# One maximum, the last narrow passes and image 0's normalisation put into other places in an eight-image convolution sequence

## The chip, the cores and the metric

The kernel runs on one NeuronCore of a Trainium2 chip. What counts is device time in microseconds (us): the time of one execution on that core. Five engines run side by side, each with its own queue in program order, and meet only at semaphores: TensorE multiplies matrices into PSUM, VectorE and ScalarE do elementwise work, GpSimd does some sums in SBUF and issues small transfers, SyncE (SP) issues most DMAs. In the profile they are PE (PEld for its weight loads), DVE, ACT, POOL and SP.

## The reference

The input is 8 images of 512 channels and 32x32 positions, all in float32. Four layers follow one another:

```python
h = group_norm(x)                                   # layer 0: 8 groups of 64 channels
q, k, v = split(qkv_w @ h + qkv_b)
h = softmax(q k / 8) v                              # 8 heads of 64 channels
for _ in range(3): h = h + 0.1 * tanh(h @ inl_w.T + inl_b)
x = x + proj_w @ h + proj_b

x = x + softmax(Wq x . Wk x) (Wv x)                 # layer 1: one head over 1024 positions

x = upfirdn(x + bias, up=2)                         # layer 2: 12 taps, rows and columns
x = leaky_relu(x, 0.2) * sqrt(2)
x = upfirdn(x, down=2)

rw = sigmoid(mean(x) @ router_w.T + router_b)       # layer 3: 8 experts, weights mixed per image
W1, W2, W3 = mix(rw, w1), mix(rw, w2), mix(rw, w3)
y = relu(bn(conv1x1(x, W1))); y = relu(bn(conv3x3(y, W2)))
x = relu(bn(conv1x1(y, W3)) + x)
```

## The kernel before

Channels lie on the 128 partitions in 4 chunks (`CC`), positions on the free axis in two halves of 512 (`HALF`). Every wide product is done in Strassen's way with seven quarter products (`product`, L554, and `in_turn`, L610): P1, C11, U2, U3, C22, C21, C12. P1 and C11 read the left half of the positions as it is; U2, U3, C22 and C21 read four sums of quarters (`T_h`, made by `quarter_sum`, L541) and sums of the weights' quarters. An f32 matmul is one row in the code and two passes in the profile.

Layers 0 to 2 run image by image (loop at the end of the `weights` pool: `layer0`, `layer1`, `between`). Image 0 starts in `first_qkv` (L807): `channel_stats` (L419) takes `bn_stats` of each chunk as it lands, `norm_factors` (L441) averages mean and variance over groups with a tiny matmul each (`gn_mean`, `gn_var`), takes Sqrt on ScalarE and makes a factor and an addend per channel, and `group_norm` scales `x` chunk by chunk on VectorE. Then come the first sums of the query weights (`first_sums`, `first_rest`), the quarter sums, and q, k and v.

The order of work is set in two ways. Under `tc.manual_schedule(engines=...)` the named engines run what is issued in the order of the code. Elsewhere a planner orders the instructions by its own estimates; it also fills between two such blocks. `first_qkv` is left to the planner.

In the last image (b = 7) layer 0 also computes the router of images 0 to 6: `early_router` (L833) is a generator with a step for the sums on VectorE, one for `logits` (a matmul with ones, then seven VectorE steps and an exp on ScalarE) and one per image for the blend operators. The loop over 64 score tiles issues one step each time once i > 2 (L1010):

```python
                if i < steps:
                    scores(i)
                if i > 2:
                    next(router, None)
                if i >= lag:
                    weighted(i - lag)
```

Layer 2 of the last image is interleaved with layer 3 of images 0 and 1. `chain` is the generator `lean_images`: the first convolution in two halves (`first`, L1652), the spread of its rows for the 3x3 convolution (`spread`), the second convolution with 4 steps and the third with one step per output chunk `oc` (both in `second`, L1666). The third convolution's matmul results go to two PSUM banks of the pool `ps_mm`, and VectorE adds them onto `z` (L1700); a bank is free when that is done.

`fine_passes` (L1364) runs 8 row passes. Each has `up` (16 small matmuls into two PSUM pairs; ScalarE makes 0.2 times each pair, VectorE takes the maximum of both, L1292), `down` for the pass before (matmuls, then two copies to `sent`, on ScalarE, the second on VectorE in odd passes; SP stores `sent`), after the fourth `turn_back` (SP loads the stored rows as `back`), and then two calls of `fill`, each of which takes one step of `chain`. In the fifth pass the second `fill` also issues the loads of image 2 (`z`, 4 DMAs; `weights`, 12 DMAs), which `first(2, 0)` reads as c_2_0 (L1656).

`last_columns` (L1471) ends layer 2: for each half `e` of the channels two `narrow` passes (matmuls from `back`; copies on VectorE), steps of `chain`, and two `channels` (transposes zT; ScalarE copies them to `z` and sums the pooled mean). After it another hand-ordered block begins with image 2's first convolution (`c1`, c_2_1), its spread, the router of image 7 (`router.sums`) and c_3_0, and then loops over images 2 to 7. Between the two blocks the planner has put c_2_1, c_3_0 and five of the first six second-convolution matmuls between the last two narrow passes.

SP's queue is in program order: a store waits at its head for its copy, and the loads behind it wait too.

Of the kernel before, what the change touches and what calls it, by code (L numbers as in the profile page):

```python
# [9 lines left out]
F32 = mybir.dt.float32  # L10
BF16 = mybir.dt.bfloat16
AF = mybir.ActivationFunctionType
ALU = mybir.AluOpType
# [4 lines left out]
P = 128  # L18
B, C, H, W = 8, 512, 32, 32
S = H * W  # L20
# [38 lines left out]
def tile_sequence(ctx: ExitStack, tc: tile.TileContext, a: dict, out: bass.AP, shifted: bool):  # L59
# [359 lines left out]
    def channel_stats(b, x):  # L419

        stats = small.tile([P, CC, 2, 6], F32, tag="stats", bufs=1, name=f"stats_{b}")
        mv = small.tile([P, CC, 2], F32, tag="mv", bufs=2, name=f"mv_{b}")
        for cc in range(CC):
            for h in range(2):
                nc.vector.bn_stats(stats[:, cc, h, :], x[:, cc, ts(h, HALF)])
            nc.vector.bn_aggr(mv[:, cc, :], stats[:, cc, :, :].rearrange("p h s -> p (h s)"))
            yield mv
# [10 lines left out]
            nc.vector.tensor_sub(be, be, m)  # L438
            bn.append((g, be))

    def norm_factors(b, mv, made):  # L441
        mean_c, var_c = mv[:, :, 0], mv[:, :, 1]
        ps = ps_sc.tile([P, S], F32, tag="scores", name=f"gn_mean_{b}")
        nc.tensor.matmul(ps[:, 0:CC], group_mean, mean_c, start=True, stop=True)
        mean = small.tile([P, CC], F32, tag="gmean", bufs=2, name=f"gmean_{b}")
        nc.vector.tensor_copy(mean, ps[:, 0:CC])
        dev = small.tile([P, CC], F32, tag="gdev", bufs=2, name=f"gdev_{b}")
        nc.vector.tensor_sub(dev, mean_c, mean)
        nc.vector.tensor_mul(dev, dev, dev)
        nc.vector.tensor_add(dev, dev, var_c)  # L450
        yield
        ps = ps_sc.tile([P, S], F32, tag="scores", name=f"gn_var_{b}")
        nc.tensor.matmul(ps[:, 0:CC], group_mean, dev, start=True, stop=True)
        mul = small.tile([P, CC], F32, tag="gmul", bufs=2, name=f"gmul_{b}")
        nc.scalar.activation(mul, ps[:, 0:CC], AF.Sqrt, bias=eps)
        nc.vector.reciprocal(mul, mul)
        nc.vector.tensor_mul(mul, mul, gn_scale)
        add = small.tile([P, CC], F32, tag="gadd", bufs=2, name=f"gadd_{b}")
        nc.vector.tensor_mul(add, mean, mul)
        nc.vector.tensor_sub(add, gn_bias, add)  # L460
        made.extend((mul, add))
        yield

# [131 lines left out]
    def all_of(gen):  # L595
        for _ in gen:
            pass
# [207 lines left out]
        tc.keep_in_program_order(nc.scalar.activation(early, eps, AF.Exp))  # L805

    def first_qkv(h, w):  # L807
        made = []
        for mv in channel_stats(0, h):
            pass  # L810
        all_of(norm_factors(0, mv, made))
        group_norm(h, *made, nc.vector)
        first_sums(*held["q"], h[:, CC - 1, 0:1])
        t = quarter_sums("h_0", h)
        w["q"] = first_rest(*held["q"])
        for key in "kv":
            w[key] = weight_sums(key, *held[key], t[3][1][:, 0:1])
        q, parts = queries(0, h, t, w)
        all_of(parts)
        nc.vector.tensor_add(row_bias, row_bias, bias2)  # L820
        w["inl"] = weight("inl", 0)
        k, parts = keys(0, h, t, w)
        for _ in range(2):
            next(parts)
        early_exp(0)
        all_of(parts)
        w["proj"] = weight("proj", 0)
        v, parts = values(0, h, t, w)
        all_of(parts)
        w["v1"] = weight("v1", 0)  # L830
        return q, k, v
# [10 lines left out]
    def layer0(b, q, k, v, w):  # L842
# [162 lines left out]
        with tc.manual_schedule(engines={engines.PE, engines.DVE, engines.Activation}):  # L1005
            router = iter(early_router() if b + 1 == B else ())
            for i in range(steps + lag):
                if i < steps:
                    scores(i)
                if i > 2:  # L1010
                    next(router, None)
                if i >= lag:
                    weighted(i - lag)
                done = i - lag - SC - 1
                for g in range(1, 2 * PAIRS, 2):
                    closing_pair(g, done - g * SC)
                for g in range(2 * PAIRS, last_g):
                    closing(g, done - g * SC)
            t_hf = sum_tiles(f"hf_{b}_0")
            name = f"inl_{b}_0"  # L1020

            def last_total():
                quarter_sum(t_hf, hf, 0, (0, 1))
                for at in range(3):
                    closing(last_g, at)
                quarter_sum(t_hf, hf, 1, (0, 1))
                quarter_sum(t_hf, hf, 0, (2, 3))
                quarter_sum(t_hf, hf, 1, (2, 3))
# [208 lines left out]
    class Layer2:  # L1237
# [34 lines left out]
            for i in range(4):  # L1272
                nc.sync.dma_start(t[:, ts(i, 4), :], src[:, ts(i, 4), :])

        def up(self, e, i):

            n = 4 * e + i
            pairs = [
                ps_sc.tile([P, S], F32, tag="scores", name=f"up_{self.b}_{n}_{p}") for p in range(2)
            ]  # L1280
            for s in range(2):
                for g in range(4):
                    part = slice(W * g, W * g + W)
                    first = 4 * i + 2 * s
                    nc.tensor.matmul(  # L1285
                        pairs[g // 2][HD * s : HD * s + HD, ts(g % 2, HALF)], up_v[part, :],
                        self.turned[e][part, first : first + 2, :], start=True, stop=True,
                    )
            fine = self.fine[n] = [tmp(f"fine_{self.b}_{n}_{p}", S) for p in range(2)]
            for ps, t in zip(pairs, fine):  # L1290
                nc.scalar.mul(t, ps, 0.2)  # L1291
                nc.vector.tensor_max(t, ps, t)  # L1292

        def down(self, e, i):

# [67 lines left out]

        def fine_passes(self, fill):  # L1364
            order = [(e, i) for e in range(2) for i in range(4)]
            for n in range(len(order) + 1):
                if n < len(order):
                    self.up(*order[n])
                if n:
                    e, i = order[n - 1]  # L1370
                    self.down(e, i)
                    if i == 3:
                        self.turn_back(e)
                fill()
                fill()

    engines = mybir.EngineType
    hand = {engines.PE, engines.DVE, engines.Activation, engines.SP}
# [80 lines left out]
    def last_rows(two, chain, loads):  # L1459
        done = 0  # L1460

        def fill():
            nonlocal done
            next(chain, None)
            done += 1
            loads(done)

        with tc.manual_schedule(engines=hand):
            two.fine_passes(fill)

    def last_columns(b, two, chain, loads):  # L1471
        with tc.manual_schedule(engines=hand):
            z = big_tile(f"z_{b}", [P, CC, S])
            for e in range(2):
                two.narrow(e, 0)
                two.narrow(e, 1)
                loads(e)
                for _ in range(2):
                    next(chain, None)
                two.channels(e, 0, z)  # L1480
                two.channels(e, 1, z)
                for _ in range(4 - 2 * e):
                    next(chain, None)
            all_of(chain)
        return z

    def load_z(b):
        t = big_tile(f"z3_{b}", [P, CC, S])
# [177 lines left out]
    def second(b):  # L1666
# [14 lines left out]
        c2(b, main, 0, False, True)  # L1681
        nc.scalar.activation(h2[:, ts(0, HALF)], main, AF.Relu, bias=bn[1][1], scale=bn[1][0])
        transform_weights(b + 1)
        yield

        def closed(oc):
            dst = zs[b][:, oc, :]
# [3 lines left out]
        for oc in range(CC):  # L1691
            scale = bn[2][0][:, oc : oc + 1]
            apart = zs[b][:, oc, :].rearrange("p (n i) -> p i n", i=2)
            at = C + 12 * P + oc * P
            for i in (1, 0):
                ps = bank(name=f"c3_{b}_{oc}_{i}")
                nc.tensor.matmul(
                    ps, wts[b][:, at : at + P], h2[:, ts(i, HALF)], start=True, stop=True
                )
                nc.vector.scalar_tensor_tensor(  # L1700
                    apart[:, i], ps, scale, apart[:, i], ALU.mult, ALU.add
                )
            if oc:
                closed(oc - 1)
            yield
        closed(CC - 1)

    LEAN = 2
# [20 lines left out]
            load_image(3)  # L1729
            next(mixing)  # L1730

    zs[B - 1] = last_columns(B - 1, two, chain, more_loads)
    redo = None
    engines = mybir.EngineType
    with tc.manual_schedule(engines={engines.PE, engines.DVE, engines.Activation}):
        c1(LEAN, 1)
        spreads[LEAN] = spread(LEAN)
        router = Router(B - 1, 1)
        router.sums()
        c1(LEAN + 1, 0)  # L1740
        for b in range(LEAN, B):
            more = b + 1 < B
            if b + 2 < B:
# [110 lines left out]
```

## Time and profile before

| | us |
|---|---|
| median of 3 runs | 3546.42 (3546.16 to 3550.63) |
| profiled execution | 3549.11 |
| its span | 3547.3 |
| TensorE busy | 3508.9 |
| VectorE busy | 2320.8 |
| ScalarE busy | 1316.9 |
| mean granted TensorE clock | 0.998 |

The span counts from the first to the last instruction; some 1.8 us of the execution lie around it. In a row of the profile, `L585 PE` is line 585 on TensorE, followed by output and input tiles and sizes. In the timeline the first number is the start and the second the length; what stands in brackets is how long the engine had been idle before it and who ended that. In the list of waits the numbers are the total, how often, and the longest. TensorE's idle time in the whole span is 38 us, 11.0 of them before its first instruction.

### The profile page before, as it was taken

How to read it: one execution, taken by the hardware profiler on the slowest of the kernel's cores; microseconds unless marked ns; L12 is line 12 of the kernel's file. 1: busy time of each engine (PE TensorE's matmuls, PEld its weight loads, DVE VectorE, ACT ScalarE, POOL GpSimd, SP SyncE). 2: the span in 40 equal slices, each digit the busy share in tenths (PEclk: the TensorE clock that was granted, in tenths of full speed). 3: DMA queues.
4: the chain of work that ended last, by engine and by line, in shares of the span. 5: the costliest groups of instructions: out<-in, count | busy, mean ns of one | idle time of the engine just before them, and what ended most of it. 6: DMA issues, size and time to landing. Idle time of an engine off the chain costs nothing.

```text
span 3547.3 us, 48514 instructions
## 1 busy us (share of the span) xinstructions
PE 3508.9 (99%) x19649; PEld 1743.1 (49%) x19649; DVE 2320.8 (65%) x3131; ACT 1316.9 (37%) x1742; POOL 109.3 (3%) x152
## 2 busy tenths in 40 slices
PE   8999999999999999999999999999999999999998
PEld 4335643474435743465534744356434744347333
DVE  4787558765686557774677656775677656765544
ACT  0632346223442236323452235422462234531443
POOL 4100000000000000000000000000000000020000
PEclk9999999999999999999999999999999999999999
DMA  5112351115311341023411152013511153332783
GB/s 205 40 31 86 101 176 43 45 54 154 117 37 65 116 159 36 29 86 115 165 39 64 57 168 87 30 70 112 182 43 43 44 154 128 123 104 74 261 297 129
DMA packets 153841, 360.89 MB, mean 102 GB/s; under 512 B 20072, under 2 KB 94840, under 8 KB 147464
## 3 DMA queue, kind: packets, MB, share of 16 engines
q1 hardware_dynamic: 150104, 342.69, 29.1%
q0 software_dynamic: 3360, 14.75, 1.1%
q8 instruction: 156, 2.56, 0.3%
q14 instruction: 77, 0.63, 0.1%
q10 hardware_dynamic: 144, 0.26, 0.0%
HBM read 226.55 MB, written 118.49 MB: 97 GB/s over the span
## 4 chain that ended last, share of the span: by engine, by line
PE 96%; DMA 1%; DVE 1%; SPq 0%; ACT 0%; issue 0%; ACTq 0%; DVEq 0%
PE scores L872 12%; PE av L917 12%; PE inl_X L585 7%; PE av_X L1226 5%; PE inl_Y L585 5%; PE inl_A L585 5%; PE av_A L1226 3%; PE av_Y L1226 3%; PE v_X L585 3%; PE proj_X L585 2%; PE k_X L643 2%; PE q_X L643 2%; PE v_X L643 2%; PE c L1598 2%; PE v_Y L585 2%; PE v_A L585 2%
## 5 line engine op out<-in xcount | busy, mean ns | idle before, releaser
L891 ACT ACTIVATE e<-scores 128x1024 f32<-128x1024 f32 x504 | 516.7, 1025 | 395.4 <-PE scores L872 368.9
L872 PE MATMUL scores<-q,k 64*64 64x512 f32 x4096 | 530.7, 591 | 0.0
L917 PE MATMUL av<-e,v 64*64 64x512 f32 x4096 | 528.7, 589 | 0.0
L901 DVE TENSOR_TENSOR accs<-accs,e 128x1024 f32<-128x1024 f32 x240 | 294.3, 1226 | 49.6 <-ACT e L891 46.0
L917 PEld LDWEIGHTS av<-e,v 64*64 64x64 f32 x4096 | 156.5, 133 | 282.3 <-issue 274.0
L872 PEld LDWEIGHTS scores<-q,k 64*64 64x64 f32 x4096 | 152.8, 133 | 289.9 <-issue 255.6
L585 PE MATMUL inl_X<-T_hf,w_inl 128*128 128x512 f32 x576 | 262.3, 593 | 1.0 <-DVE inl_U L739 1.0
L1292 DVE TENSOR_TENSOR fine<-up,fine 128x1024 f32<-128x1024 f32 x128 | 150.8, 1220 | 105.4 <-ACT fine L1291 105.4
L1291 ACT ACTIVATE fine<-up 128x1024 f32<-128x1024 f32 x128 | 124.2, 1021 | 162.8 <-PE up L1285 161.6
L585 PEld LDWEIGHTS inl_X<-T_hf,w_inl 128*128 128x128 f32 x576 | 108.3, 190 | 141.4 <-issue 109.7
L585 PE MATMUL inl_A<-hf,w_inl 128*128 128x512 f32 x384 | 174.4, 597 | 0.0
L728 ACT ACTIVATE inl_U<-inl_U,inl_b 128x512 f32<-128x512 f32 x96 | 66.8, 719 | 287.3 <-DVE inl_U L743 287.3
L938 DVE RECIPROCAL inv<-av 128x256 f32<-128x256 f32 x80 | 139.0, 1745 | 0.0
L739 DVE TENSOR_TENSOR inl_U<-inl_X,inl_P 128x512 f32<-128x512 f32 x96 | 61.8, 686 | 106.6 <-PE inl_X L585 106.6
L899 DVE TENSOR_TENSOR accs<-e,e 128x1024 f32<-128x1024 f32 x48 | 59.6, 1243 | 99.5 <-ACT e L891 80.5
L1226 PE MATMUL av_A<-v,eT 128*128 128x256 f32 x512 | 122.6, 383 | 0.0
L585 PEld LDWEIGHTS inl_A<-hf,w_inl 128*128 128x128 f32 x384 | 71.5, 190 | 96.8 <-issue 86.1
L1226 PE MATMUL av_X<-v,eT 128*128 128x256 f32 x512 | 114.0, 381 | 0.0
L1263 ACT COPY wide<-wide 128x1024 f32<-128x1024 f32 x62 | 59.8, 1015 | 139.6 <-PE wide L1255 139.6
L1115 ACT ACTIVATE eT<-scores 128x512 f32<-128x512 f32 x128 | 66.1, 602 | 115.4 <-PE scores L412 115.4
L1226 PEld LDWEIGHTS av_X<-v,eT 128*128 128x128 f32 x512 | 96.6, 190 | 19.3 <-DVE av_U L1200 6.5
L901 DVE TENSOR_TENSOR acc<-acc,e 128x1024 f32<-128x1024 f32 x80 | 96.8, 1210 | 8.4 <-ACT e L891 7.6
(400 smaller groups left out, 5513.3 us busy)
## 6 DMA issues: line engine op xcount, KB each, us to landing
x<-in_x_dram SPq DMA_DIRECT2D x64, 512.0 KB
across_u<-wide SPq DMA_DIRECT2D x128, 256.0 KB
turned<-across_u SPq DMA_DIRECT2D x64, 512.0 KB
back_u<-sent SPq DMA_DIRECT2D x256, 128.0 KB
back<-back_u SPq DMA_DIRECT2D x32, 1024.0 KB
w_v<-stored_u_v SPq DMA_DIRECT2D x14, 1792.0 KB
out_dram<-z SPq DMA_DIRECT2D x31, 512.0 KB
spill_u<-z SPq DMA_DIRECT2D x28, 512.0 KB
```

Source lines behind the costliest of these rows:

```text
L585: nc.tensor.matmul(dst, lhs, rhs, start=(opens and s == 0 and cc == 0), stop=(cc == 1 and s == rows), skip_group_check=True,)
L643: nc.tensor.matmul(dst, lhs, rhs, start=(what in opens and s == 0 and cc == 0), stop=(cc == 1 and s == rows), skip_group_check=True,)
L728: nc.scalar.activation(t, ps, AF.Tanh, bias=inl_b[:, c : c + 1])
L872: nc.tensor.matmul(ps[r][rows[c]], k[rows[r], oc, jc * P + c * HD : jc * P + c * HD + HD], q[rows[r], oc, ts(sh, HALF)], start=True, stop= ...
L891: nc.scalar.activation(e, pair, AF.Exp, scale=HD ** -0.5)
L901: nc.vector.tensor_add(accs[g], accs[g], e)
L917: nc.tensor.matmul(avs[g][r][rows[c]], v[rows[r], jc, ts(2 * oc + c, HD)], e[rows[r], ts(c, HALF)], start=(jc == 0), stop=(jc == SC - 1),)
L938: nc.vector.reciprocal(copies[g][:, at], totals[g][:, at])
L1226: nc.tensor.matmul(ps[:, ts(s, QR)], left[:, j, at : at + P], right[:, j, :], start=(what in ("P1", "U2", "C22") and s == 0 and j == 0), s ...
L1291: nc.scalar.mul(t, ps, 0.2)
L1292: nc.vector.tensor_max(t, ps, t)
L1598: nc.tensor.matmul(ps, wts[b][:, at : at + P], spreads[b][:, i, 16 * ky : 16 * ky + HALF], start=(start and ky == 0), stop=(stop and ky == ...
```

## The change

Four places are edited.

- `norm_factors` can do a part of the chunks; `first_qkv` does chunks 0 and 1 and then chunks 2 and 3, in an order by hand on TensorE, VectorE and ScalarE: statistics of the later chunks between the steps of the first part, and scaling by half chunks.
- The router's steps in layer 0 come at odd i only.
- `second` yields True where the next steps are the third convolution's; `fine_passes` then puts the second maximum of the pass after the first of its two fills. This holds in two passes, the fifth and the sixth (e = 1, i = 0 and 1).
- The first steps of the block after `last_columns` become a function `then`, called at the end of `last_columns` within its hand-made order.

```diff
-    def norm_factors(b, mv, made):
-        mean_c, var_c = mv[:, :, 0], mv[:, :, 1]
+    def norm_factors(b, mv, made, part=slice(0, CC)):
+        n, apart = part.stop - part.start, part.stop - part.start < CC
+        name = f"{b}_{part.start}"
+        mean_c, var_c = mv[:, part, 0], mv[:, part, 1]
+        ps = ps_sc.tile([P, S], F32, tag="scores", name=f"gn_mean_{name}")
+        nc.tensor.matmul(ps[:, 0:n], group_mean, mean_c, start=True, stop=True)
+        if apart:
+            yield
...
         yield
...
+        nc.tensor.matmul(ps[:, 0:n], group_mean, dev, start=True, stop=True)
+        nc.scalar.activation(mul, ps[:, 0:n], AF.Sqrt, bias=eps)
+        if apart:
+            yield
         nc.vector.reciprocal(mul, mul)
...
     def first_qkv(h, w):
-        made = []
-        for mv in channel_stats(0, h):
-            pass
-        all_of(norm_factors(0, mv, made))
-        group_norm(h, *made, nc.vector)
+        def normed(made, first, half):
+            for i in range(2):
+                at = h[:, first + i, ts(half, HALF)]
+                by = [t[:, i : i + 1] for t in made]
+                nc.vector.tensor_scalar(at, at, *by, ALU.mult, ALU.add)
+
+        with tc.manual_schedule(engines={engines.PE, engines.DVE, engines.Activation}):
+            stats, upper, lower = channel_stats(0, h), [], []
+            mv = next(stats)
+            next(stats)
+            one = norm_factors(0, mv, upper, slice(0, 2))
+            two = norm_factors(0, mv, lower, slice(2, CC))
+            next(one)
+            next(stats)
+            for _ in range(2):
+                next(one)
+            next(stats)
+            next(two)
+            next(one)
+            normed(upper, 0, 0)
+            for _ in range(2):
+                next(two)
+            normed(upper, 0, 1)
+            next(two)
+            for half in range(2):
+                normed(lower, 2, half)
         first_sums(*held["q"], h[:, CC - 1, 0:1])
...
-                if i > 2:
+                if i > 2 and i % 2:
                     next(router, None)
...
-        def up(self, e, i):
+        def up(self, e, i, apart):
...
                 nc.scalar.mul(t, ps, 0.2)
-                nc.vector.tensor_max(t, ps, t)
+                if not apart or t is fine[0]:
+                    nc.vector.tensor_max(t, ps, t)
+            return lambda: nc.vector.tensor_max(fine[1], pairs[1], fine[1])
...
         def fine_passes(self, fill):
             order = [(e, i) for e in range(2) for i in range(4)]
+            apart, second = None, None
             for n in range(len(order) + 1):
                 if n < len(order):
-                    self.up(*order[n])
+                    second = self.up(*order[n], apart)
...
                 fill()
-                fill()
+                if apart and n < len(order):
+                    second()
+                apart = fill()
...
         def fill():
             nonlocal done
-            next(chain, None)
+            apart = next(chain, None)
             done += 1
             loads(done)
+            return apart
...
-    def last_columns(b, two, chain, loads):
+    def last_columns(b, two, chain, loads, then):
...
             all_of(chain)
-        return z
+            zs[b] = z
+            then()
...
         transform_weights(b + 1)
-        yield
+        yield True
...
-            yield
+            yield oc + 1 < CC
...
-    zs[B - 1] = last_columns(B - 1, two, chain, more_loads)
-    redo = None
-    engines = mybir.EngineType
-    with tc.manual_schedule(engines={engines.PE, engines.DVE, engines.Activation}):
+    router = Router(B - 1, 1)
+
+    def then():
         c1(LEAN, 1)
         spreads[LEAN] = spread(LEAN)
-        router = Router(B - 1, 1)
         router.sums()
         c1(LEAN + 1, 0)
+
+    last_columns(B - 1, two, chain, more_loads, then)
+    redo = None
+    with tc.manual_schedule(engines={engines.PE, engines.DVE, engines.Activation}):
```

In the instruction order TensorE gets two more tiny matmuls, VectorE eight more small steps and eight scalings of half a chunk in place of four of a whole one, ScalarE one more Sqrt. No DMA is added or moved in SP's order; on GpSimd a few weight sums and stores change places with their neighbours. At the end, c_2_1, c_3_0 and the first six second-convolution matmuls follow the last transposes.

More of the change, by code (lines that the diff above doesn't have):

```diff
@@ L439, in batch_norms @@
             bn.append((g, be))
-    def norm_factors(b, mv, made):
-        mean_c, var_c = mv[:, :, 0], mv[:, :, 1]
[L443 to L447, printed above, removed]
+    def norm_factors(b, mv, made, part=slice(0, CC)):
[6 more added lines that the diff above has]
+            yield
+        mean, dev, mul, add = (
+            small.tile([P, CC], F32, tag=tag, bufs=2, name=f"{tag}_{name}")[:, 0:n]
+            for tag in ("gmean", "gdev", "gmul", "gadd")
+        )
+        nc.vector.tensor_copy(mean, ps[:, 0:n])
         nc.vector.tensor_sub(dev, mean_c, mean)
@@ L451, in norm_factors @@
         yield
[L452 to L455, printed above, removed]
+        ps = ps_sc.tile([P, S], F32, tag="scores", name=f"gn_var_{name}")
+        nc.tensor.matmul(ps[:, 0:n], group_mean, dev, start=True, stop=True)
+        nc.scalar.activation(mul, ps[:, 0:n], AF.Sqrt, bias=eps)
+        if apart:
+            yield
         nc.vector.reciprocal(mul, mul)
-        nc.vector.tensor_mul(mul, mul, gn_scale)
-        add = small.tile([P, CC], F32, tag="gadd", bufs=2, name=f"gadd_{b}")
+        nc.vector.tensor_mul(mul, mul, gn_scale[:, part])
         nc.vector.tensor_mul(add, mean, mul)
-        nc.vector.tensor_sub(add, gn_bias, add)
+        nc.vector.tensor_sub(add, gn_bias[:, part], add)
         made.extend((mul, add))
```

## The prediction

> **What bounds the kernel now.** I read the page's first part, then TensorE's waits (who waited for whom), then the timeline around each long wait.
>
> ```profile
> PE 3508.9 (99%) x19649; PEld 1743.1 (49%) x19649; DVE 2320.8 (65%) x3131; ACT 1316.9 (37%) x1742; POOL 109.3 (3%) x152
> ...
> PE gn_mean L444 <- DVE mv L426: 11.0, 1, 11.0
> PE router L276 <- DVE parts L271: 4.1, 2, 2.1
> PE c L1697 <- DVE z L1700: 3.3, 2, 2.0
> PE c L1656 <- DMA weights<-mixed_u: 2.2, 1, 2.2
> PE q_A L585 <- DVE x L468: 2.0, 1, 2.0
> ...
> PE c L474 <- DVE narrow L1344: 0.8, 1, 0.8
> ```
>
> TensorE is busy 3508.9 of 3547.3 us, so all that an edit of order can win lies in 38 us of idle time, and in matmul passes that run slowly. The change aims at five of these waits. The passes matter too: a 128x512 pass normally starts 0.43 us after the one before (two passes per f32 matmul), but the table of windows shows three stretches at half rate, each after a gap:
>
> ```profile
> 3322.00:3324.00 2.00, 2.00 (x3) 0.67 (x2) 0.68 (x2) 1.15 (x1) 0.00 (x0) 0.50 0.89 232
> 3343.00:3345.00 2.00, 2.00 (x3) 0.70 (x3) 0.97 (x1) 0.00 (x0) 0.00 (x0) 0.50 0.67 185
> 3394.00:3396.00 2.00, 2.00 (x4) 0.93 (x3) 0.11 (x1) 0.00 (x0) 0.00 (x0) 0.50 1.03 414
> ```
>
> (PEclk is the third number from the right.) Such a stretch lasts some 3.4 us (the six passes after 3392.44 take 4.15 us instead of 2.6), so it costs 1.6 to 1.7 us.
>
> **A. Image 0's normalisation in parts.** Now: the last `bn_aggr` ends at 10.93, two tiny matmuls and ten small VectorE steps follow, `x` is scaled from 14.15, the first pass of q_A starts at 15.02. New chain, from durations of this trace (small step 0.2 spacing; 1024-wide scaling 0.81 long, 0.72 spacing, so I estimate 512-wide at 0.54 and 0.45): two chunks' statistics end at 7.4, gn_mean at 8.3; VectorE does chunk 2 until 9.4, four small steps until 10.2, chunk 3 (landed 9.34) until 11.7; gn_var and the Sqrt (0.27) are over by 11.3. Four small steps: 12.5; half a chunk scaled: 13.05; q_A can start at 13.1, **1.9 us earlier**. Its weights do not stop it: the ScalarE operand that lands after them is there by 13.2. Then the price. The second gn_var (0.59 cold) sits after q_A's first two matmuls. ScalarE's second Sqrt waits for it behind the q_P copy, then VectorE needs four small steps and a half chunk: the lower rows are ready 2.6 us after the first two matmuls end, about when P1's other two (and gn_var) end. So hardly a wait there. VectorE gains 8 small steps (1.6 us) and 0.7 us of scaling, and stands idle 1.4 us; its T_h sums end at 25.1 instead of 23.9. U2 then needs them at 24.4, when 24.1 suffices, and a k_A matmul is put ahead of it. GpSimd's weight sums start 1.2 us later; those of w_k were ready at 32.7 and are first read at 49, so they stay hidden.
>
> What decides is the rate of the first passes:
>
> ```profile
> 20.30 0.34 PEld L585 LDWEIGHTS q_A<-x,w_q 128*128 128x128 f32 x1 [0.52 <-issue]
> 21.16 0.22 PEld L585 LDWEIGHTS q_A<-x,w_q 128*128 128x128 f32 x1 [0.52 <-issue]
> 21.62 0.19 PEld L585 LDWEIGHTS q_A<-x,w_q 128*128 128x128 f32 x1 [0.24 <-issue]
> ```
>
> Passes are 0.85 us apart until 21.2, then 0.43: 6.2 us of half rate, though PEclk reads 1.00 there. The Trainium skill ("TensorE: Matmul & The Clock Gate", Part 1) says that the clock starts at half rate and is released after a free-running window of about 3.4 us of sustained activity. It agrees with the three stretches; for the start it speaks against the change, because gn_var now stands inside the first window. If that window still counts as busy, A gives 1.9 less gn_var, up to 2.3; if not, half rate lasts one window more and A lies between +0.7 and -1.0, by where the windows fall. I take **+1.0**, ends -1.0 and +2.3.
>
> **B. Router stepped every second time.** At i=4 TensorE reaches `router` at 2965.0 and waits until 2967.11, because the parts come on VectorE behind two 1.2 us sums. Now the weighted product of i=4 and the scores of i=5 (2 x 0.86) come first: 2.10 becomes about 0.5. VectorE's seven `rw` steps come after one more 1.2 us sum, so the router's PSUM buffer is free at 2970.0, when scores 7 asks for it at 2970.1; ScalarE's exp of scores 6 ends at 2971.3, read at 2971.8. No new wait, by 0.1 and 0.5 us. The blend operators end 7 steps later, but are used only after step 64. **+1.55** (1.2 to 2.1).
>
> **C. The second maximum amid the third convolution's fill.**
>
> ```profile
> 3317.67 1.98 PE L1697 MATMUL c<-h,weights 128*128 128x512 f32 x4
> 3321.66 3.59 PE L1697 MATMUL c<-h,weights 128*128 128x512 f32 x4 [2.01 <-DVE z L1700]
> ...
> 3324.68 1.00 SPq L1321 DMA_DIRECT2D back<-back_u  x2
> ...
> 3329.47 14.24 SPq L1540 DMA_DIRECT2D weights<-mixed_u  x12
> ...
> 3342.53 5.30 PE L1656 MATMUL c<-z,weights 128*128 128x512 f32 x8 [2.25 <-DMA weights<-mixed_u]
> ```
>
> Moving one 1.2 us maximum behind the first two `z` steps frees the banks at 3320.5 instead of 3321.6: the waits 2.01 and 1.29 become 0.95 and 0.25, and the half rate of 3322-3325 may go: TensorE is 2.1 (waits) to 3.8 us earlier. But it then meets c_2_0, which waits for image 2's data. That stream (2 MB back, 0.5 out, 2 z, weights) runs from 3324.68 at 300 to 373 GB/s and does not get faster. It starts when the rows of `sent_3` are stored, and their VectorE copy (3320.27) now stands behind one maximum instead of two: 1.07 us earlier. The same chain holds dn_7, whose ScalarE copy waits for sends queued on SP behind these weights. So TensorE idles some 4 to 5 us at c_2_0 and goes on 1.07 us earlier. The gap makes half rate certain (before: also there); some cases run into dn_7's 0.45 us of slack. **+0.9**, ends 0 and +1.1.
>
> **D. Narrow passes in one hand-made order.**
>
> ```profile
> 3372.67 1.09 PE L1338 MATMUL narrow<-back,dn_h 64*32 64x512 f32 x16
> ...
> 3388.43 1.75 PE L1356 MATMUL zT<-ident,narrow 128*128 128x128 f32 x14 [0.16 <-DVE narrow L1346]
> ...
> 3392.22 0.36 PE L276 MATMUL router<-parts,ones 128*128 128x8 f32 x2 [2.04 <-DVE parts L271]
> 3392.44 4.36 PE L1598 MATMUL c<-spread,weights 128*128 128x512 f32 x6
> ```
>
> Now, from 3372.67 to the end of those six passes (3396.59): 23.9 us. New order: narrow 1,0 and 1,1 (2.05), wait for the two 0.6 us copies (0.5), wait for the 1.22 us copy (1.0), transposes (1.75), c_2_1 and c_3_0 (16 passes, 6.87), c2 (12 passes, 5.15), router (0.25), c2 (6 passes, 2.6): 20.1. The 2.04 us router wait goes, since its parts now have 12 us; what is new is 1.5 us of waits in the narrow pass, less than the 2.10 us of the first router, after which the passes kept their 0.43. Gain **3.8**, of which 1.6 is the half-rate stretch; without it 2.2. ScalarE: the `rim` step now follows two z evictions and is free at 3379.4, c_2_1 ends at 3381.4; spread's first sum is there at 3382.9, needed at 3384.8. SP's order is unchanged; the `out` stores come 7 us earlier, so later loads do too. The second half of `back` landed at 3368.45, read now at 3373.7.
>
> By the skill's rule (half rate after an idle window of about 3.4 us) no 2.0 us gap would cost more than itself, and D would be 2.2 in every run; by the row a gap of 2.0 did, when it fell inside one window.
>
> **Sum.** Profiled execution: 3549.1 (span 3547.3 and 1.8 around it) - 1.0 - 1.55 - 0.9 - 3.8 = 3541.8. The median of the runs, 3546.4, is 2.7 lower; I read that as a run without D's half-rate stretch and with a shorter slow start: 3546.4 - 1.0 - 1.55 - 0.9 - 2.2 = 3540.8. I say **3541.0**.
>
> **Rivals.**
> 1. *The loads do not hold c_2_0*: C then gives 2.1 to 3.8. For it: the wait shown is only 2.2. Against: the DMA share is 1.04 and 0.90 from 3330 to 3342.5, with the loads issued as earlier ones land. Time 3538.5. Chance 0.16.
> 2. *The start gives nothing and the narrow pass brings half rate*: A at -1.0 and D at 2.2 - 1.7. For it: gn_var in the first window, 1.5 us of gaps amid small matmuls. Time 3544.5. Chance 0.18.
> 3. *Slower by the clock*: the new gaps (gn_var, c3, the 4 to 5 us before c_2_0, the narrow pass) each cost half-rate windows of 1.7 us; from the fourth beyond my sum on, the gain is gone: 3547.8. Against: the c3 gaps get shorter, and part of c_2_0's is behind dn_7. Chance 0.04.
> 4. The order itself does what it says: the instruction order shows every move above.
> The main case keeps 0.62, its own range 3539 to 3543.
>
> **Numbers.** Range 3537.8 to 3544.6. What can be told from no change is about 0.2%, 7.1 us: faster means under 3539.3. That is most of rival 1 (0.13) and the low tail of the main case (0.13): 0.26; slower 0.03.
>
> **What would show it.** q_A's first pass at 13.1; passes 0.43 apart from about 18 or only from 21 and later; router's first wait 0.5; c3's waits under 1 us each; c_2_0 waiting for DMA 4 to 5 us; narrow's waits 1.5 and none at the second router. I am wrong if c_2_0's wait does not grow, or if half-rate stretches appear in new places.

## The result and the profile after

| | before | after |
|---|---|---|
| median of 11 runs each, us | 3548.49 (3546.16 to 3552.86) | 3539.86 (3538.33 to 3541.4) |
| profiled execution, us | 3549.11 | 3538.69 |
| its span, us | 3547.3 | 3536.8 |

The ratio of the runs is 0.9974, with a 95% interval of 0.9964 to 0.9983: the changed kernel is 8.6 us faster. The forecast of 3541.0 is 1.1 us off and inside its range, but the gain was put at 5.4 us (3546.42 to 3541.0; 7.3 in the profiled execution). The likeliest case, a change too small to be told from none, with a chance of 0.71, did not come.

The page's first part for the changed kernel (busy time of each engine, share of the span, instructions):

```profile
PE 3503.7 (99%) x19653; PEld 1744.1 (49%) x19653; DVE 2320.5 (66%) x3143; ACT 1316.6 (37%) x1743; POOL 109.7 (3%) x152
```

TensorE is busy 5.2 us less than before with four more tiny matmul records, so half of the 10.5 us of span came from passes that run faster, and half from idle time. The list of TensorE's waits in the changed kernel (who waited for whom: us in total, times, longest):

```profile
PE gn_mean L446 <- DVE mv L426: 7.3, 1, 7.3
PE c L1690 <- DMA weights<-mixed_u: 5.6, 1, 5.6
PE gn_var L459 <- DVE gdev L456: 2.4, 1, 2.4
...
PE zT L1385 <- DVE narrow L1375: 1.2, 1, 1.2
...
PE c L1731 <- DVE z L1734: 0.9, 1, 0.9
PE gn_mean L446 <- DVE gmul L463: 0.9, 1, 0.9
PE dn L1332 <- ACT sent L1338: 0.8, 1, 0.8
PE q_A L591 <- DVE x L818: 0.6, 1, 0.6
```

The third convolution's 3.3 became 0.9, and the two routers' waits have left the head of the list. The wait for image 2's data grew from 2.2 to 5.6. The first router before and after:

```profile
2967.11 0.40 PE L276 MATMUL router<-parts,ones 128*128 128x56 f32 x2 [2.10 <-DVE parts L271]
...
2964.07 0.40 PE L276 MATMUL router<-parts,ones 128*128 128x56 f32 x2 [0.38 <-DVE parts L271]
```

The start of q_A in the changed kernel:

```profile
12.96 0.50 PEld L591 LDWEIGHTS q_A<-x,w_q 128*128 128x128 f32 x2 [0.70 <-DVE x L818]
...
16.83 0.19 PEld L591 LDWEIGHTS q_A<-x,w_q 128*128 128x128 f32 x1 [0.24 <-issue]
17.26 0.19 PEld L591 LDWEIGHTS q_A<-x,w_q 128*128 128x128 f32 x1 [0.24 <-issue]
```

Its first pass comes at 12.96 instead of 15.02, and passes are 0.43 us apart well before 17, where the kernel before needed until 21.2.

The timeline of the changed kernel around the wait for image 2's data (start, us, engine, line, operation; in brackets the idle time ahead of it and what ended it):

```profile
3315.87 1.99 PE L1731 MATMUL c<-h,weights 128*128 128x512 f32 x4 [0.88 <-DVE z L1734]
...
3318.88 1.00 SPq L1350 DMA_DIRECT2D back<-back_u  x2
...
3319.85 4.10 PE L1731 MATMUL c<-h,weights 128*128 128x512 f32 x8
...
3323.60 15.13 SPq L1574 DMA_DIRECT2D weights<-mixed_u  x12
...
3337.28 5.23 PE L1690 MATMUL c<-z,weights 128*128 128x512 f32 x8 [5.55 <-DMA weights<-mixed_u]
...
3338.84 1.77 SPq L1341 DMA_DIRECT2D back_u<-sent  x4
...
3342.67 1.07 ACT L1338 COPY sent<-dn 128x512 f32<-128x512 f32 x2 [9.95 <-DMA back_u<-sent]
...
3343.30 1.57 PE L1332 MATMUL dn<-fine,dn_v 64*32 64x512 f32 x16 [0.80 <-ACT sent L1338]
```

Ahead of c_2_0 TensorE is 8.6 us earlier than before (A and B are 4.7 of that; the third convolution's sixteen passes, the last twelve of them shown, run with one short wait and at full rate), but the weights stream that began at 3329.47 and took 14.24 us now begins at 3323.60 and takes 15.13. What TensorE won it spends at 3337.28, and the gap brings half rate: eight passes take 5.23 us. Behind them dn_7 waits for a ScalarE copy that waits for the sends of 3338.84, queued on SP behind the same weights.

The timeline of the changed kernel's narrow passes:

```profile
3367.74 1.95 PE L1367 MATMUL narrow<-back,dn_h 64*32 64x512 f32 x32
...
3371.40 1.75 PE L1385 MATMUL zT<-ident,narrow 128*128 128x128 f32 x14 [1.23 <-DVE narrow L1375]
...
3385.00 0.28 PE L276 MATMUL router<-parts,ones 128*128 128x8 f32 x2
3385.14 2.82 PE L1632 MATMUL c<-spread,weights 128*128 128x512 f32 x6
```

The six passes behind the router take 2.82 us, not 4.36, and the router waits for nothing.

Cut at five places, the two profiles compare as follows. The limits are starts of TensorE's groups in the timelines: the scores of the last image's layer 0; 200 passes of its weighted values later; dn_7; narrow_1_0; the end of the six passes behind the second router; the last matmul.

| stretch | before | after | difference | forecast |
|---|---|---|---|---|
| up to the scores (A) | 2958.77 | 2955.74 | 3.03 | 1.0 |
| router in layer 0 (B) | 47.64 | 45.99 | 1.65 | 1.55 |
| to dn_7 (C) | 341.87 | 341.58 | 0.29 | 0.9 |
| to narrow_1_0 | 24.40 | 24.44 | -0.04 | 0 |
| narrow passes (D) | 24.12 | 20.22 | 3.90 | 3.8 |
| to the last matmul | 142.00 | 140.97 | 1.03 | 0 |

The differences make 9.86 us; the other 0.65 of the span's 10.5 lies behind the last matmul's start. That tail takes from 7.4 to 9.1 us in the five profiles of before and of A, B, C and D alone, so the 0.65 is put down to no part.

### The profile page after: what moved, and what is told of

The parts are those of the page before. It is cut to its first block, busy times and chain, and to the rows that moved or that the text cites. A ratio compares the mean times of both kernels' runs of the same rounds, so it can differ in the third digit from the quotient of the medians.

```text
span 3536.8 us, 48540 instructions
## 1 busy us (share of the span) xinstructions
PE 3503.7 (99%) x19653; PEld 1744.1 (49%) x19653; DVE 2320.5 (66%) x3143; ACT 1316.6 (37%) x1743; POOL 109.7 (3%) x152
## 4 chain that ended last, share of the span: by engine, by line
PE 97%; DMA 1%; DVE 1%; ACT 0%; SPq 0%; issue 0%; POOL 0%; DVEq 0%; ACTq 0%; POOLq 0%
PE scores L899 12%; PE av L944 12%; PE inl_X L591 7%; PE av_X L1253 5%; PE inl_Y L591 5%; PE inl_A L591 5%; PE av_A L1253 3%; PE av_Y L1253 3%; PE v_X L591 3%; PE proj_X L591 2%; PE k_X L649 2%; PE c L1632 2%; PE q_X L649 2%; PE v_X L649 2%; PE v_Y L591 2%; PE up L1312 2%
```

## The experiments

Every kernel was timed in five rounds beside the kernel before, whose medians were 3548.5 to 3549.1, so medians of kernels that were not timed together can be compared to within some 0.6 us; each left one profile. The stretches of the table above are given for each as they are needed.

**One part of the change at a time.** Four kernels are the kernel before with one part each. A alone takes `norm_factors` and `first_qkv` of the change; B, C (with what passes `apart` and calls `second`) and D (with `then` as in the change) are, by their main lines:

```diff
-                if i > 2:
+                if i > 2 and i % 2:
...
-                nc.vector.tensor_max(t, ps, t)
+                if not apart or t is fine[0]:
+                    nc.vector.tensor_max(t, ps, t)
...
-    zs[B - 1] = last_columns(B - 1, two, chain, more_loads)
+    last_columns(B - 1, two, chain, more_loads, then)
```

> Part A alone on the kernel before (image 0's normalisation in two parts, nothing else). Theory 1, read from the trace of the changed kernel: first pass of q_A 2.0 us earlier (at 13.0 instead of 15.02), and the first stretch at half rate ends by 16 instead of 21.2, because gn_var costs the first window only 0.3 us of idle time; layer 0's scores then start 3.0 us earlier and the median falls by 2 to 3.5 us. Rival, as the prediction had it: gn_var spoils the first window, half rate lasts past 18, and the median moves by -1.0 us at most.

> Part B alone on the kernel before (router stepped at every second step of layer 0). Theory: the 2.10 us wait of the first router matmul becomes 0.4, nothing new waits, the median falls by 1.7 us. Rival: a stretch at half rate hung on that gap in some executions, then 2.3 to 3.4 us; or the PSUM buffer or exp arrives late (0.1 and 0.5 us to spare by the prediction), then under 1 us.

> Part C alone on the kernel before (second maximum of a row pass behind the first two steps of the third convolution). Theory 1: the waits amid the third convolution fall from 3.3 to about 0.9 us, but the DMA wait before c_2_0 grows by about as much (2.3 to 4.5 or more), and the last copy of the sends comes only 0.3 us earlier, so the median falls by 0.3 us (0 to 1.1). Rival: the image's loads do not hold the pass and the median falls by 2 to 4 us.

> Part D alone on the kernel before (narrow passes, first convolution and router in one hand-made order). Theory 1: the 2.04 us wait of the second router and the half-rate stretch behind it go, and 1.2 us of new wait comes at the transposes: 3.9 us between the narrow pass and the first six passes of image 2's second convolution in the profile, 2.2 to 3.9 us in the median. Rival: the half-rate stretch is only of some executions and the new wait brings one of its own, then 0.5 to 1.5 us.

| kernel | median, us | ratio to before, 95% | scores | router | to dn_7 | narrow |
|---|---|---|---|---|---|---|
| before, its profile | 3548.85 (41 runs) | | 2958.77 | 47.64 | 341.87 | 24.12 |
| A alone | 3545.97 | 0.9993 (0.9985 to 1.0001) | 2955.80 | 49.34 | 343.13 | 24.28 |
| B alone | 3547.18 | 0.9997 (0.9989 to 1.0005) | 2958.99 | 46.00 | 342.19 | 22.58 |
| C alone | 3546.18 | 0.9994 (0.9985 to 1.0002) | 2957.53 | 47.64 | 340.74 | 24.09 |
| D alone | 3545.25 | 0.9990 (0.9982 to 0.9998) | 2958.39 | 47.64 | 342.92 | 20.22 |

Only D's interval keeps clear of 1; the medians fall by 2.9, 1.7, 2.7 and 3.6 us, 10.8 in sum against 9.0 for all four together (3548.85 to 3539.86). C's 2.7 is far above the 0.3 expected, but its interval reaches to no change, and its own stretch is only 1.1 us shorter in its profile. The stretches say more than the medians, because stretches that no edit touched differ too: the narrow passes take 24.1 to 24.3 in the profiles of before, A and C alone but 22.58 in that of B alone, with the same wait ahead of them. Two timelines show it. B alone, at the second router (nothing of it is edited there):

```profile
3391.11 0.36 PE L276 MATMUL router<-parts,ones 128*128 128x8 f32 x2 [2.04 <-DVE parts L271]
3391.33 2.82 PE L1598 MATMUL c<-spread,weights 128*128 128x512 f32 x6
```

A alone, at the first router (nothing edited there either):

```profile
2964.14 0.40 PE L276 MATMUL router<-parts,ones 128*128 128x56 f32 x2 [2.10 <-DVE parts L271]
2964.47 1.27 PE L944 MATMUL av<-e,v 64*64 64x512 f32 x8
2965.50 1.95 PE L899 MATMUL scores<-q,k 64*64 64x512 f32 x8
```

After the same gap of 2.04 us the six passes here take 2.82 us, where they took 4.36 in the profile of before; and behind the first router, where before kept full rate, A alone shows scores of 1.95 us instead of 1.04. So a gap of 2.0 to 2.1 us brings a half-rate stretch in some executions and none in others. The trace's record of the granted clock shows where the two differ: every half-rate stretch but the last, which the end of the run cuts, is a multiple of 3.413 us long. In each profile the ends of all of them lie on one grid with that spacing, and a stretch comes where the gap lies inside one cell of the grid, between two of its points (in A alone: rate halved from 2965.25, gap from 2962.04 to 2964.14, cell from 2961.84). B alone at the second router: the gap from 3389.08 to 3391.12 is cut by a grid point at 3390.05, and nothing happens. The grid lies elsewhere in each execution. Over the profiles of the kernels that still have these gaps (two routers, one in the third convolution), 10 of 17 gaps brought a stretch of 3.413 us at half rate, worth 1.7 us: those that had 1.97 us or more in one cell; the seven that had 1.90 or less did not. The gaps ahead of c_2_0 and dn_7, which the count leaves out, agree: at full rate, a cell with 2.09 us or more of idle time was followed by half rate, one with 1.84 or less was not. No kernel here places a gap on purpose, so the rule rests on this fit. By these limits a gap of 2.05 us laid anywhere on the grid would bring the stretch in some 46% of places (an estimate, with 1.94, the middle of the two limits, as the bound).

That gives B a value of 1.65 or 3.35 and D one of 2.36 or 3.9. It may also be why the kernel before spreads over 6.7 us in 11 runs and the changed one, with none of these gaps, over 3.1. That is not shown: the warm start below has none of them either and spreads over 5.9 in nine runs.

For A the theory's second half fell. Its own profile has q_A at 12.80 and full rate from 16.13, as expected; but three later kernels that keep the changed start have full rate only from 17.60, 18.59 and 18.71 (below).

**Image 2's loads earlier.** Edit to the changed kernel, which moves the loads ahead of the 2 MB brought back:

```diff
-    last_rows(two, chain, lambda n: load_image(2) if n == 10 else None)
+    last_rows(two, chain, lambda n: load_image(2) if n == 8 else None)
```

> The changed kernel with image 2's loads issued two fills earlier, ahead of the 2 MB that the row passes bring back. Theory (this DMA stream holds c_2_0): its wait of 5.55 us and the half-rate stretch behind it go, the wait for sends at dn_7 too, so narrow_1_0 starts some 7 us earlier than in the changed kernel (5.6 of wait, 1.4 to 1.7 of half rate) unless the rows brought back are then late for their narrow pass; time 3532 to 3535. Rival (something else, such as the rows sent, sets c_2_0's place): under 1 us, 3539.

And the same with part C undone (`if True:` for `if not apart or t is fine[0]:`, no `second()`):

> The same early loads, with part C undone (both maxima ahead of the third convolution's steps again). Theory: with no load to wait for at c_2_0, the 2.1 us of waits that C took away come back in full, so this is 2.1 us slower than the early loads with C (3.8 where a half-rate stretch falls on the 2.0 us gap): C was worth little only because the loads took it back. Rival (C is worth little in itself): within 0.7 us of the early loads with C.

Measured: 3534.83 (ratio 0.9960, 0.9946 to 0.9974) and 3534.63 (0.9962, 0.9948 to 0.9976). The early loads win 5.0 us over the changed kernel, so it was the stream that held c_2_0; of the 7 us expected, 5.2 are there at dn_7, and the half rate behind its new wait takes 1.6 of them until the narrow pass. But C was worth nothing on top. The timeline of the early loads with C:

```profile
3326.77 1.01 SPq L1350 DMA_DIRECT2D back<-back_u  x2
...
3327.88 1.26 SPq L1723 DMA_DIRECT2D out_dram<-z  x1
...
3329.23 2.04 SPq L1341 DMA_DIRECT2D back_u<-sent  x4
...
3332.52 3.70 PE L1690 MATMUL c<-z,weights 128*128 128x512 f32 x8
...
3338.36 1.07 ACT L1338 COPY sent<-dn 128x512 f32<-128x512 f32 x2 [4.78 <-DMA back_u<-sent]
...
3339.00 2.14 PE L1332 MATMUL dn<-fine,dn_v 64*32 64x512 f32 x16 [2.78 <-ACT sent L1338]
```

c_2_0 follows without a wait and at full rate, and dn_7 now waits 2.78 us, for the copy of the pass before. That copy needs one of the two buffers of `sent`, which the sends of 3329.23 read. They went out behind 2 MB brought back (3326.77) and 0.5 MB of output (3327.88), and the trace has the last of them landed at 3338.26, 0.1 us before the copy. Without C TensorE reaches dn_7 at 3340.53 and waits for nothing there. So the literal expectation (2.1 us) failed, and the rival's number came, by another gate in the same traffic.

**The gate taken away too.** The rows brought back are first read by the narrow pass some 7 us behind dn_7; in this kernel they come two row passes later. It also holds the next two experiments' edits (the first convolution ahead of the transposes; passes on zeros at the start, which nothing reads).

With `late = (1, 1)` in `last_rows`:

```diff
-                    if i == 3:
-                        self.turn_back(e)
+                    if (e, i) in (late, (1, 3)):
+                        self.turn_back(0 if (e, i) == late else 1)
```

> The changed kernel with four edits: image 2's loads two fills earlier; the first 2 MB brought back issued two row passes later (behind the sends and stores that ran into them with the early loads alone, and that then held dn_7 by 2.8 us); the first convolution ahead of the transposes; and half as many passes on zeros at the start as in the warm start (three instructions, two, and one, none ahead of q_A). Theory: neither c_2_0 nor dn_7 waits for transfers, so dn_7 starts about 7.5 us sooner after layer 0 than in the changed kernel; 1.4 us from the narrow passes, 1.4 us or more from the start: 3528 to 3532. Rival: the rows brought back later are late for narrow_0 (read some 7 us after dn_7) and the pass waits there instead: 3533 to 3536.

> The same with part C undone. Theory: with no transfer behind the row passes to wait for, C's 2.1 us of waits count in full: 2.1 us slower than with C, 3.8 where a half-rate stretch falls on the 2.0 us gap. Rival: another gate near dn_7 or narrow_0 takes it back, within 0.7 us.

Measured: 3529.86 (3529.35 to 3530.16; ratio 0.9945, 0.9931 to 0.9958) and without C 3532.54 (0.9954, 0.9940 to 0.9967). Timeline of the first:

```profile
3314.66 1.98 PE L1742 MATMUL c<-h,weights 128*128 128x512 f32 x4 [0.88 <-DVE z L1745]
...
3330.45 3.70 PE L1701 MATMUL c<-z,weights 128*128 128x512 f32 x8
3334.08 1.24 PE L1341 MATMUL dn<-fine,dn_v 64*32 64x512 f32 x16
3335.25 5.42 PE L1643 MATMUL c<-spread,weights 128*128 128x512 f32 x12
3340.60 1.95 PE L1376 MATMUL narrow<-back,dn_h 64*32 64x512 f32 x32
```

And of the second:

```profile
3315.66 3.24 PE L1742 MATMUL c<-h,weights 128*128 128x512 f32 x4 [2.01 <-DVE z L1745]
...
3324.54 1.98 PE L1742 MATMUL c<-h,weights 128*128 128x512 f32 x4 [1.29 <-DVE z L1745]
...
3337.85 1.25 PE L1341 MATMUL dn<-fine,dn_v 64*32 64x512 f32 x16
```

No group from c_2_0 to the narrow pass waits in either, and now C counts in full: 333.57 against 337.46 us from the router to dn_7, 3.9 us, of which some 1.6 is the half rate behind the 2.01 us gap (four passes in 3.24 us instead of 1.98, and the row pass behind them). In the medians it is 2.7, since the last stretch gives 0.8 back (143.35 against 142.53 us; more waits for the experts' loads of `mix_last`). C's small value in the changed kernel is thereby shown to be the doing of the transfers: the loads, and with these moved, the rows brought back. The whole is 10 us faster than the changed kernel.

**The wait that D made.** Edit to the changed kernel: `c1(LEAN, 1)` is called in `last_columns` behind the second half's narrow passes, not in `then`.

> The changed kernel with the first convolution c_2_1 ahead of the last narrow pass's transposes instead of behind them. Theory (the 1.23 us at the transposes is the wait that D newly made, hidden by any work put there): the wait goes, the median falls by 1.2 us, to 3538.6; in the trace 19.0 instead of 20.2 us from narrow_1_0 to the end of the six passes. Rival: spread, which needs c_2_1 through ScalarE, or z gets late instead and the second convolution waits: no gain.

Measured: 3537.66 (0.9969, 0.9957 to 0.9981), and 18.75 us in the narrow stretch against 20.22. The median fell by 2.2 us, 1.0 more than expected; the stretch accounts for 1.47. The 1.23 us at the transposes was open time that any ready work fills; nothing behind it got late.

**The start's clock.** The changed kernel with passes on zeros in TensorE's idle time (`busy(n)` issues n 128x512 matmuls of the tile `seen`, still zero, with `ones`):

```diff
+            busy(6)
             next(one)
             next(stats)
             next(one)
+            busy(4)
             next(one)
             next(stats)
+            busy(1)
             next(two)
+            busy(1)
             next(one)
             normed(upper, 0, 0)
```

The lean warm start has 3, 2, 1 and 0 for 6, 4, 1 and 1. The kernel before gets `busy(7)` ahead of gn_mean and `busy(2)` ahead of q_A.

> The changed kernel with twelve 128x512 passes on a tile of zeros put into TensorE's idle time before q_A (six ahead of the first gn_mean, four ahead of gn_var, one each ahead of the second gn_mean and of q_A); they add work that nothing reads. Theory (the start's half rate lasts until one whole window of about 3.4 us has been busy, wherever that window falls): q_A's passes are 0.43 us apart from its first one on, the scores of layer 0's last steps start 1.4 us earlier than in the changed kernel's trace, and the median falls by 1.4 to 3. Rival (the rate comes from elsewhere, such as the arrival of the weights): the first passes stay 0.85 us apart and the time stays.

> The changed kernel with half as many passes on zeros at the start as in the warm start, so that they end before gn_mean, gn_var and the second gn_mean want TensorE (each of the warm start's instructions was two passes, and q_A came 3.1 us later for it). Theory: q_A's first pass at about 13.0 as in the changed kernel and 0.43 us to the next one; the scores start 1.2 to 3 us earlier than in profiles of the changed kernel's start (2955.7 to 2957.1), and the median falls by 1.2 to 2.5. Rival: q_A is late again or the clock falls back to half rate in the gaps left: no gain.

> The kernel before with passes on zeros in TensorE's idle time at its start (seven instructions ahead of gn_mean, two ahead of q_A; nothing reads them), the counterpart of the changed kernel's lean warm start. With the clock released on both sides, what is left between the two is part A without the clock. Theory: q_A's first pass at 15.0 to 15.4 with 0.43 us to the next one; the scores start at 2955.7 to 2956.3, 1.5 to 2.1 us later than the 2954.2 of the lean warm start and 1.9 to 3.1 us earlier than in the profiles without the zeros (2957.5 to 2959.0): A is worth 1.5 to 2.1 in the normalisation itself, and the rest of the 3.0 between the first two profiles is where the clock's windows fell. Rival: A's 3.0 is all its own and the scores start at 2957.2.

| kernel | median, us | q_A's first pass | full rate from | scores |
|---|---|---|---|---|
| before; B, C, D alone | | 15.02; 15.12, 15.12, 15.37 | 21.20; 21.09, 18.87, 20.36 | 2958.77; 2958.99, 2957.53, 2958.39 |
| after; A alone | | 12.96; 12.80 | 15.81; 16.13 | 2955.74; 2955.80 |
| early loads; without C; convolution first | | 12.54; 12.96; 12.43 | 18.71; 18.59; 17.60 | 2956.58; 2957.07; 2955.72 |
| warm start | 3539.26 | 16.05 | 7.96 | 2957.64 |
| lean warm start | 3538.26 | 12.39 | 5.55 | 2954.18 |
| before, warm | 3546.59 | 15.19 | 7.23, half again 14.05 to 17.47 | 2956.80 |

The warm start missed: an instruction on f32 is two passes, so twice the intended work stood ahead of q_A, which came 3.1 us late. Even so its passes ran 0.43 us apart from the first one. The lean form keeps that, with q_A's first pass at 12.39. Weight loads of q_A in its timeline, whose spacing is that of the passes:

```profile
12.92 0.19 PEld L591 LDWEIGHTS q_A<-x,w_q 128*128 128x128 f32 x1 [0.24 <-DVE gmean L453]
13.35 0.19 PEld L591 LDWEIGHTS q_A<-x,w_q 128*128 128x128 f32 x1 [0.24 <-issue]
```

Its median is 1.6 us under the changed kernel's, inside what was expected (the two were not timed together; measured from the kernel before on each side it is 2.2). The kernel before with zeros fell back to half rate from 14.05 to 17.47, which the expectation did not have: the 3.413 us before that held two tiny matmuls with 1.3 us of gaps ahead of them. The stretch covers q_A's first 2.28 us, 1.14 us of time. Without it the scores would start at 2955.66. The lean warm start is 1.5 us ahead of that, and the two fastest kernels, which start in the same way, 1.15 and 1.3 (2954.51 and 2954.38): A is worth 1.2 to 1.5 apart from the clock.

How the second gn_var bears on the rate is told by the weight loads of the early-load kernel, where the half rate lasted longest with the changed start:

```profile
14.41 0.34 PEld L591 LDWEIGHTS q_A<-x,w_q 128*128 128x128 f32 x1 [0.52 <-issue]
15.26 0.34 PEld L459 LDWEIGHTS gn_var<-gdev,group_mean 128*128 128x128 f32 x1 [0.52 <-issue]
16.11 0.34 PEld L459 LDWEIGHTS gn_var<-gdev,group_mean 128*128 128x128 f32 x1 [0.52 <-issue]
...
18.25 0.34 PEld L591 LDWEIGHTS q_A<-x,w_q 128*128 128x128 f32 x1 [0.52 <-issue]
18.91 0.19 PEld L591 LDWEIGHTS q_A<-x,w_q 128*128 128x128 f32 x1 [0.33 <-issue]
```

Full rate comes at 18.71, so the deciding stretch of 3.413 us began at 15.30, and gn_var's matmuls, from 16.11 to 16.40, belong to it. It released the clock all the same. That does not show that they count as busy: they take 0.3 us at most, and in the changed kernel a stretch with 0.57 us of idle time released it. (There gn_var's matmuls come at 16.18, behind the release.) The stretch before, from 11.88, had 0.66 us ahead of q_A and did not count.

## Why the prediction came out as it did

**A was mis-sized: 1.0 forecast, 3.0 between the two profiles.** The step that failed is "if not, half rate lasts one window more and A lies between +0.7 and -1.0", with the middle value drawn from it. In five profiles with the changed start the second gn_var either stood behind the release (this one and A alone) or inside the window that brought it. The first pass came at 12.96 where 13.1 was worked out, and the lower rows made little wait. Of the 3.0, 1.2 to 1.5 us is A's own (the warm starts). The rest is the clock: half rate lasted 2.85 us from q_A's first pass in this profile and 6.18 in the one before, a difference worth 1.66 us. That is mostly chance: over the profiles it lasts 3.75 to 6.18 with the old start and 2.85 to 6.17 with the new one. The scores start on average at 2958.42 (four profiles) and 2956.18 (five), each set scattering over some 1.4 us, so A is worth about 2.2, the forecast's upper end. The Trainium skill ("TensorE: Matmul & The Clock Gate", Part 1) calls its window of about 3.4 us free-running and the number of slow passes different from run to run; the table above agrees with that. It makes one profile's start a draw, not a duration to add up with.

**B was right**: 1.65 for 1.55, router waiting 0.38 for 0.5. It left out that the old gap also brings half rate in some executions (2 of 5 profiles), another 1.7 us there.

**C was right in its mechanism, and small as said.** c_2_0's wait grew to 5.55 (4 to 5 forecast). The stream began 5.8 us earlier (3324.68 to 3318.88), of which 4.7 are A's and B's, so C moved it by 1.1 (1.07 forecast). In the pair C is 0.29 for 0.9: from its start to c_2_0 the stream took 0.55 us longer than before, which the sum held constant, and dn_7's own wait grew from 0.45 to 0.80.

Not all of the growth from 2.25 to 5.55 is C's. In the profiles of A, B and D alone, where the third convolution's gap brought no half rate, the wait is 4.10 to 4.37 already; with the half rate it is 2.25 and 2.29 (before, and before with zeros). So a half-rate stretch ahead of this wait costs nothing: the wait takes it back.

Over all profiles C is worth 1.0: the stretch to dn_7 averages 342.4 in five kernels without C and 341.4 in five with it, without the early loads. Rival 1 (3538.5, loads that do not hold) is refuted for this kernel by the early loads.

**D was right** at both ends: 3.9 with the half rate in the old order, 2.36 without it; 1.23 us of new wait for 1.5.

**The base was off.** The median of three runs, 3546.42, was read as an execution without D's half-rate stretch and with a short slow start. 41 runs gave 3548.85, and that half-rate stretch stood in 4 of 5 profiles with the old order. So 2.2 for D in the second sum was too little, and the base 2.4 too low against the 41 runs. That the time came out within 1.1 us is therefore luck: the gain was 3.2 us larger than forecast (8.6 for 5.4), and the base of three runs was 2.1 lower than the median of the eleven. The 1.0 us after the narrow passes was not forecast; that stretch takes from 140.5 to 142.5 in thirteen of the fourteen profiles whatever the order (143.35 in the fastest kernel), so it is not put down to the change.

## What to carry to other kernels

Where transfers end a wait, making the waiting engine faster buys only as much as it moves the start of the transfers; move them first (5 us here), look for the next gate in the same queue (another 2.8), and only then count the engine's edit, which was then worth 2.7 instead of about 1. A gap of about 2 us on TensorE is dearer than its length, by 1.7 us in about half of the executions (10 of 17 gaps here), so cost it at about 3, unless a later wait takes the loss back, and take no single profile's half-rate stretches as given. Work on zeros in idle time at the start pays if it ends before the first real matmul wants the engine.

## What the runs showed of the hardware

- Half-rate stretches lie on a grid of 3.413 us that stands elsewhere in each execution. Of the 17 gaps counted, those with 1.97 us or more in one cell brought one each time, those with 1.90 or less never. The Trainium skill ("TensorE: Matmul & The Clock Gate", Part 1) has the rate halved after an idle window of about 3.4 us; here the runs decide against it.
- At the start a window with 0.57 us of idle time released the clock (12.40 to 15.81 in the changed kernel); ones with 0.64 and 0.66 us ahead of q_A (the kernel before, the early loads) did not.
- Whether tiny matmuls count as busy stays open. In the kernel before with zeros the window from 10.64 to 14.05 had 1.31 us without any matmul and brought half rate back; with its two tiny matmuls (four passes) counted as idle it is 1.94, between the two limits above.
- The granted clock in the table of windows reads 1.00 while passes are 0.85 us apart at the start; the spacing of the weight loads shows the slow start, the clock's column does not: the record behind it begins with the first stretch at full rate.
